# Three drains of TensorE in each pass of a gather-and-scatter kernel

## The chip, the core and the metric

The kernel runs on one core of one Trainium2 chip. The metric is the device time of one execution in microseconds, as the median of several runs. The engines are named as the profile names them: PE is TensorE's matrix unit (PEld its weight loads), DVE is VectorE, ACT is ScalarE, POOL is GpSimd, and SP is SyncE, whose queue issues most DMAs.

## What is computed

One layer of a graph network with 12500 nodes and 400000 edges, 128 features each, in float32:

```python
h = jnp.maximum(_layernorm(x, axis=-1), 0.0)
# inside the layer, on that h:
h = h @ W_in2f.T
Wij = smu(f_ij @ W_f1.T + b_f1) @ W_f2.T + b_f2     # f_ij: 400000 x 20
Wij = Wij * rcut_ij[:, None]
x_ij = h[idx_j] * Wij                                # gather by dst
agg = jax.ops.segment_sum(x_ij, idx_i, num_segments=h.shape[0])   # sum by src
out = smu(agg @ W_o1.T + b_o1) @ W_o2.T + b_o2
x = x + out
```

`smu` is a smooth activation; the kernel makes it from Gelu and a linear term. The edges are sorted by dst, so 128 neighbouring edges read few rows of h. Their src is in no order.

## The kernel before

The edges are cut into 3125 tiles of 128. Four tiles make a group (`GRP`), two groups a super (`SUP`), and one pass of the main loop works on four successive groups at once, each at another stage. There are 782 groups, so 782 passes. The nodes are cut into 98 bins of 128 (`NB`). The messages of the edges go in two steps: first every message row is scattered to DRAM, into a buffer sorted by bin; later the rows of a bin are fetched again and summed on TensorE. The supers are cut into ten epochs (`PARTS`). While one epoch's messages are scattered, an earlier epoch's are summed, bin by bin, with three DRAM buffers in turn.

The order of the instructions on PE, DVE, ACT and SP is the order in which the code writes them (`manual_schedule`). Each engine goes through its list in order, and the framework puts semaphores between them. In pass p the loop (lines 1139 to 1174) calls these helpers:

- `turn` of group p (L707): four 128x128 transposes of the messages `mt` into the PSUM tile `pt`. For the groups that are kept aside (the last two epochs, from `EARLY` on) it is a product with `w_o1` (L709) instead.
- `send` of group p: ScalarE writes the row's place in its bin into the last column of `ms` (L718 or L720), then copies the four transposes out of `pt`, scaled by the edge weight (L723). GpSimd scatters each of the four tiles with one indirect DMA (L738). `ms` has six buffers. Groups from `EARLY` on are stored in order instead (L725) and scattered after the loop.
- `number` of group p+1: VectorE makes the four columns of scatter addresses `ix` (L620).
- `weigh` of p+1 (L686): the second filter product, 512 columns, into `pw`; it reads `sm`.
- `gather` of p+1 (L667): a one-hot product that picks the rows of h, into `ph`.
- `take` of p+1 (L675): ScalarE copies `ph` to `hg`.
- `parts`, first half: some products that sum an earlier epoch's bins (`pg`, L799), about ten a pass in all.
- `mix` of p+1 (L696): VectorE makes `mt` from `pw` and `hg`.
- `hide` of p+2 (L633): the first filter product into `pu`; `bend` (L641): ScalarE's Gelu `ge` of it; `smooth` (L649): VectorE's `sm` from both.
- `count` of p+2 (L578, L580, L581): three products that count, for each edge, its place in its bin, into `pc`; `read` (L608): VectorE takes them out as `sl`.
- `pick_part` of p+3 (L531, L532): ScalarE's one-hot tile `oh`; `bins` of p+3 (L564): VectorE's `so`, four steps that count on.
- `parts`, second half.

Each of `pt`, `pw`, `ph`, `pu` and `pc` has one PSUM buffer. So TensorE's transposes of the next group wait until ScalarE's copies (L723) have read `pt`, and they wait for `mt`. The sums' products need rows that SP has fetched (L769) and a comparison `se` of VectorE (L783); when a set of bins is done, VectorE adds it to `agg` (L812).

After the loop the kept groups are loaded and scattered while the last epochs are summed; then the output products, the old x and the bias are added and stored. A branch with a slow general form (`flag > 0`) stands behind and isn't taken with these inputs.

Of the kernel before, what the change touches and what calls it, by code (L numbers as in the profile page):

```python
# [43 lines left out]
def gnn_kernel(  # L44
# [19 lines left out]
    nc = tc.nc  # L64
# [239 lines left out]
    with tc.tile_pool(name="ld", bufs=4) as ld, \  # L304
# [173 lines left out]
        def at(p):  # L478
            return seq[p] if p < len(seq) else NG

        def sup_at(p):
            return flow[p] if p < len(flow) else NS
# [5 lines left out]
        def load(s):  # L488
            if s >= NS:
                return  # L490
            t0, nt = sups[s]
            e0, n = t0 * P, nt * P
            fb = fbufs[place_of[s] % NF]
            if s > 0:
                nc.sync.dma_start(fb[0:R, :n], f_t[:, e0:e0 + n])
            loaded[s] = (fb,)
            if s > 2:
                targets(s)
# [38 lines left out]
        def s_of(g):  # L537
            return g // PER
# [32 lines left out]
        def count(g):  # L571

            if g >= NG:
                return
            n = groups[g][1]
            before, so = bins_of.pop(g)
            pc = ps1.tile([P, GRP, P], F32, name="pc")[:, :, 0:NB]
            nc.tensor.matmul(pc[:, :n], tri, so[:, :n], start=True, stop=False, skip_group_check=True)  # L578
            if n > 1:
                nc.tensor.matmul(pc[:, 1:n], rest_h, so[:, :n - 1], start=False, stop=False, skip_group_check=True)  # L580
            nc.tensor.matmul(pc[:, 0], rest_h, before, start=False, stop=True, skip_group_check=True)  # L581
            counts[g] = pc
            if g + 1 == BY:
                pt = ps1.tile([P, GRP * P], F32, name="ph")[:, :NB]
                nc.tensor.matmul(pt, ones_h, so[:, n - 1], start=True, stop=True)
                mm = cnt.tile([P, 2], F32, name="mm")
                nc.vector.tensor_reduce(mm[:, 0:1], pt[:, :NB - 1], op=ALU.max, axis=AX.X)
                nc.vector.tensor_scalar(bad[:, 3:4], mm[:, 0:1], float(ZMIN[0]), None, op0=ALU.is_gt)
            if g + 1 in first or g + 1 == NG:

                k = epoch[g // PER]
                pt = ps1.tile([P, GRP, P], F32, name="ph")[:, 0, :NB]
                nc.tensor.matmul(pt, ones_h, so[:, n - 1], start=True, stop=True)
                mm = cnt.tile([P, 2], F32, name="mm")
                nc.vector.tensor_reduce(mm[:, 0:1], pt, op=ALU.max, axis=AX.X)
                nc.vector.tensor_reduce(mm[:, 1:2], pt[:, :NB - 1], op=ALU.min, axis=AX.X)
                i = 4 + 2 * k
                nc.vector.tensor_scalar(bad[:, i:i + 1], mm[:, 0:1], float(CAP[k]), None, op0=ALU.is_gt)
                nc.vector.tensor_scalar(bad[:, i + 1:i + 2], mm[:, 1:2], float(ZMIN[k]), None, op0=ALU.is_lt)
# [11 lines left out]
        def number(g):  # L611
            if g >= NG:
                return
            (t, n), k = groups[g], epoch[g // PER]
            t0, hic = begins[k]
            if s_of(g) < EARLY:
                ix = cnt.tile([P, GRP], I32, name="ix", bufs=8)
            else:
                ix = ix_kept[:, t - kept_tile:t - kept_tile + n]
            nc.vector.scalar_tensor_tensor(ix[:, :n], slots.pop(g)[:, :n], BIG + CAP[k] - 1, hic[:, t - t0:t - t0 + n],  # L620
                                           op0=ALU.min, op1=ALU.add)
            taken[g] = ix
# [21 lines left out]
        def smooth(g):  # L644
            if g >= NG:
                return
            n = groups[g][1] * P
            sm = edge.tile([P, GRP * P], F32, name="sm")
            nc.vector.scalar_tensor_tensor(sm[:, :n], units_of.pop(g)[:, :n], LIN, hidden[g][:, :n],  # L649
                                           op0=ALU.mult, op1=ALU.add)  # L650
            hidden[g] = sm
# [3 lines left out]
        def gather(g):  # L655

            if g >= NG:
                return
            n = groups[g][1] * P
            o = g % PER * GRP * P  # L660
            oh, hw = onehot[g // PER], loaded[g // PER][2]
            ph = ps1.tile([P, GRP * P], F32, name="ph")
            if g // PER < FEW // SUP:
                for q in range(3):
                    nc.tensor.matmul(ph[:, :n], hw[:, q * D:(q + 1) * D], oh[:, o:o + n], start=(q == 0), stop=(q == 2))
            else:
                nc.tensor.matmul(ph[:, :n], hw[:3 * WIN, g % PER, :], oh[:3 * WIN, o:o + n], start=True, stop=True)  # L667
            rows_of[g] = ph

        def take(g):  # L670
            if g >= NG:
                return
            n = groups[g][1] * P
            hg = edge.tile([P, GRP * P], F32, name="hg")
            nc.scalar.activation(hg[:, :n], rows_of[g][:, :n], AF.Copy)  # L675
            rows_of[g] = hg
# [23 lines left out]
        def turn(g):  # L700

            n = groups[g][1]
            pt = ps1.tile([P, GRP, P], F32, name="pt")
            mt = mixed.pop(g)
            for j in range(n):
                if s_of(g) < EARLY:
                    nc.tensor.transpose(pt[:, j, :], mt[:, j * P:(j + 1) * P], ident)  # L707
                else:
                    nc.tensor.matmul(pt[:, j, :], mt[:, j * P:(j + 1) * P], w_o1, start=True, stop=True)  # L709
            mixed[g] = pt  # L710

        def send(g):

            t, n = groups[g]
            ms = msg.tile([P, GRP, ROW], F32, name="ms")
            m = epoch[s_of(g)] // BUFS
            if m:
                nc.scalar.activation(ms[:, :n, P], lo_b[:, t:t + n], AF.Identity, bias=mark[:, m:m + 1])  # L718
            else:
                nc.scalar.activation(ms[:, :n, P], lo_b[:, t:t + n], AF.Copy)  # L720
            pt = mixed.pop(g)
            for j in range(n):
                nc.scalar.activation(ms[:, j, 0:P], pt[:, j], AF.Copy, scale=w_sb[:, t + j:t + j + 1])  # L723
            if s_of(g) >= EARLY:
                nc.scalar.dma_start(kept_rows[:, t - kept_tile:t - kept_tile + n, :], ms[:, :n, :])  # L725
                return
            scatter(g, ms)

        def scatter(g, ms):

            ix = taken.pop(g)
            for j in range(groups[g][1]):
                scatter_tile(g, ms, ix, j)
# [103 lines left out]
        def parts(upto):  # L837
            nonlocal done
            while done < upto:
                add(summing, *work[done])  # L840
                done += 1
# [236 lines left out]
        def step():  # L1078

            nonlocal taken_steps, slot, apart_by  # L1080
            if opening:
                apart_by += 1
                if apart_by % 2 == 0:
                    opening.pop(0)()
                return
            slot += 1
            while taken_steps < COUNT and taken_steps * 3 * (eps_of[0][1] * PER - 22) < slot * COUNT:
                steps[taken_steps]()
                taken_steps += 1
# [49 lines left out]
        for p in range(len(seq)):  # L1139
            g = seq[p]  # L1140
            s = g // PER
            if p == (FEW // SUP - 3) * PER:
                assert not opening
            if p % PER == 0:
                load(sup_at(p // PER + 3))
            if s < EARLY:
                k = chores(g)
            else:
                lo = hi = done
            if p > 1 and p != SLACK:  # L1150
                turn(at(p - (p > SLACK)))
                send(at(p - (p > SLACK)))
            step()
            number(at(p + 1))
            weigh(at(p + 1))
            gather(at(p + 1))
            take(at(p + 1))
            parts(lo + (hi - lo) // 2)
            mix(at(p + 1))
            if p == 0:  # L1160
                turn(at(1))
                send(at(1))
                pick_part(at(2))
            step()
            hide(at(p + 2))
            bend(at(p + 2))
            count(at(p + 2))
            smooth(at(p + 2))
            pick_part(at(p + 3))
            bins(at(p + 3))  # L1170
            read(at(p + 2))
            parts(hi)
            step()
            assert k == 0 or taken_steps == COUNT
# [282 lines left out]
```

## Time and profile before

| | us |
|---|---|
| median of 3 runs (5183.92 to 5208.39) | 5191.76 |
| the profiled execution | 5192.84 |
| its span in the trace | 5190.7 |
| its mean granted TensorE clock | 0.887 |
| busy: PE / PEld / DVE / ACT / POOL | 3896.6 / 2442.9 / 3349.5 / 2957.4 / 3042.1 |

A timeline row has the start, the time, the engine, the source line, the operation, what it writes and reads, how many like it follow each other, and in brackets the idle time of the engine before it with what ended that idle time. "issue" there means that nothing which the profile shows ended it, "remote" that a semaphore ended it which the profile can put down to no instruction. Ends of PE's rows are modelled; the starts are recorded. A row with a count (x4) has the first one's start and the time that all of them cover. In the stage table the figures behind the window are its length, then the busy time of PE, PEld, DVE, ACT and POOL, each with its number of instructions, then the granted clock, the DMA engines' share and GB/s.

### The profile page before, as it was taken

The page shows a single profiled execution, that of the slowest core. Times are in us where ns is not written, and L with a number is a line of the kernel's source. Part 1 is how long each engine was busy: PE and PEld are TensorE (multiplying, and loading weights), DVE is VectorE, ACT ScalarE, POOL GpSimd, SP SyncE. Part 2 cuts the span into 40 slices and gives each one's busy share as a digit, 9 for nine tenths or more (in the row PEclk, how much of TensorE's full clock was granted, in tenths as well). Part 3 has the DMA queues.
Part 4 walks back from the last instruction along what each step waited for, and adds up shares of the span by engine and source line. Part 5 has one row for each costly group of instructions (what it writes and reads, how often), then busy time and mean ns, then how long its engine had stood idle before and what let it go on. Part 6 is the DMA issues. An engine that isn't in the chain of part 4 may idle for free.

```text
span 5190.7 us, 69995 instructions
## 1 busy us (share of the span) xinstructions
PE 3896.6 (75%) x18475; PEld 2442.9 (47%) x18475; DVE 3349.5 (65%) x7364; ACT 2957.4 (57%) x7286; POOL 3042.1 (59%) x3170
## 2 busy tenths in 40 slices
PE   7667767777777777777777777777778877777456
PEld 3233334444444444444444444545455555545446
DVE  6675656666666666666666666666667767667236
ACT  6567866666565565666566666655556655555001
POOL 5666665555555555555565555555656665555554
PEclk9888888988898989989898989999989999989678
DMA  5644434544444443343444344444444444444566
GB/s 158 169 138 139 141 112 147 145 146 145 139 133 122 117 118 116 118 119 115 116 125 117 118 118 131 128 129 127 124 131 145 143 128 147 140 122 147 191 195 199
DMA packets 509824, 708.03 MB, mean 136 GB/s; under 512 B 174382, under 2 KB 362815, under 8 KB 509289
## 3 DMA queue, kind: packets, MB, share of 16 engines
q1 hardware_dynamic: 401992, 484.14, 33.2%
q0 software_dynamic: 100112, 207.06, 12.1%
q10 hardware_dynamic: 7312, 12.29, 0.6%
q8 instruction: 147, 2.41, 0.2%
q14 instruction: 261, 2.13, 0.2%
HBM read 409.48 MB, written 293.71 MB: 135 GB/s over the span
## 4 chain that ended last, share of the span: by engine, by line
PE 49%; DVE 17%; ACT 12%; issue 11%; another core or an unknown queue 10%; DMA 1%; ACTq 0%; POOL 0%; DVEq 0%; POOLq 0%
PE pw L686 14%; PE pg L799 13%; PE pu L633 10%; ACT ms L723 5%; DVE mt L696 5%; DVE sm L649 4%; PE ph L667 3%; DVE se L783 3%; PE pt L707 3%; ACT hg L675 3%; ACT ge L641 2%; DVE so L564 2%; PE pc L581 1%; PE pc L578 1%
## 5 line engine op out<-in xcount | busy, mean ns | idle before, releaser
L738 POOL DMA_INDIRECT buf<-ms,ix x2944 | 2826.0, 960 | 1974.5 <-ACT ms L723 1196.9
L686 PE MATMUL pw<-sm,w_f 128*128 128x512 f32 x1562 | 1024.6, 742 | 771.9 <-DVE sm L649 479.1
L799 PEld LDWEIGHTS pg<-se,rw 128*128 128x128 f32 x8036 | 1153.0, 207 | 450.6 <-issue 372.6
L799 PE MATMUL pg<-se,rw 128*128 128x128 f32 x8036 | 1245.6, 295 | 134.1 <-issue 101.3
L723 ACT ACTIVATE ms<-pt,w_sb 128x128 f32<-128x128 f32 x3121 | 879.5, 363 | 816.5 <-PE pc L581 294.4
L696 DVE SCALAR_TENSOR_TENSOR mt<-pw,b,hg 128x512 f32<-128x512 f32 x781 | 584.0, 748 | 790.5 <-ACT hg L675 585.8
L564 DVE SCALAR_TENSOR_TENSOR so<-irow_ps,hi_f,so 128x98 f16<-128x98 f32 x2936 | 931.4, 317 | 80.3 <-DVE so L564 2.3
L633 PE MATMUL pu<-f,w_f 128*128 128x512 f32 x1562 | 904.6, 664 | 0.0
L641 ACT ACTIVATE ge<-pu 128x512 f32<-128x512 f32 x781 | 472.2, 605 | 740.3 <-remote 224.0
L649 DVE SCALAR_TENSOR_TENSOR sm<-pu,ge 128x512 f32<-128x512 f32 x781 | 535.0, 685 | 477.0 <-ACT ge L641 269.3
L686 PEld LDWEIGHTS pw<-sm,w_f 128*128 128x128 f32 x1562 | 261.2, 210 | 926.6 <-DVE sm L649 553.0
L707 PE MATMUL pt<-ident,mt 128*128 128x128 f32 x2940 | 468.0, 283 | 266.6 <-ACT ms L723 208.7
L675 ACT ACTIVATE hg<-ph 128x512 f32<-128x512 f32 x781 | 472.6, 605 | 289.5 <-PE ph L667 85.2
L783 DVE TENSOR_TENSOR se<-irow_ps,rw 128x1536 f32<-128x1536 f32 (+1 forms) x345 | 587.9, 1704 | 71.9 <-remote 28.3
L532 ACT ACTIVATE oh<-oh,onesb 128x512 bf16<-128x512 bf16 x780 | 562.6, 721 | 26.2 <-ACT oh L531 0.9
L531 ACT ACTIVATE oh<-rbc,nrow 128x512 bf16<-128x512 uint8 x762 | 553.3, 726 | 0.0
L707 PEld LDWEIGHTS pt<-ident,mt 128*128 128x128 f32 x2940 | 341.8, 145 | 312.9 <-ACT ms L723 243.2
L608 DVE TENSOR_REDUCE sl<-pc 128x4 f32<-128x392 f32 x782 | 435.5, 557 | 67.1 <-PE ph L667 22.9
L667 PE MATMUL ph<-oh,hw 126*128 126x512 bf16 x762 | 337.7, 443 | 0.0
L633 PEld LDWEIGHTS pu<-f,w_f 128*128 128x128 f32 x1562 | 292.2, 221 | 81.3 <-issue 66.1
L812 DVE TENSOR_TENSOR agg<-agg,pg 128x512 f32<-128x512 f32 (+1 forms) x200 | 134.4, 672 | 281.2 <-remote 178.1
L578 PE MATMUL pc<-so,tri 128*128 128x392 f16 x736 | 254.4, 346 | 20.6 <-DVE sl L608 13.6
(218 smaller groups left out, 2120.6 us busy)
## 6 DMA issues: line engine op xcount, KB each, us to landing
rw<-buf SPq DMA_DIRECT2D x292, 774.0 KB
buf<-zero SPq DMA_DIRECT2D x146, 387.0 KB
rbc<-rel_dram SPq DMA_DIRECT2D x389, 128.0 KB
buf<-ms,ix POOLq DMA_INDIRECT x2944
rw<-buf SPq DMA_DIRECT2D x49, 645.0 KB
f<-in_f_t SPq DMA_DIRECT2D x390, 80.0 KB
hw<-h_dram SPq DMA_DIRECT2D x762, 31.5 KB
kept_rows<-ms ACTq DMA_DIRECT2D x45, 258.0 KB
```

What stands on the lines that cost most here:

```text
L564: nc.vector.scalar_tensor_tensor(so[:, j], irow_ps[:, :NB], hi_f[:, t + j:t + j + 1], so[:, j - 1] if j else before, op0=ALU.is_equal, op1 ...
L633: nc.tensor.matmul(pu[:, :n], w_f1, loaded[g // PER][0][:, o:o + n], start=True, stop=True)
L641: nc.scalar.activation(ge[:, :n], units_of[g][:, :n], AF.Gelu, scale=ZS)
L649: nc.vector.scalar_tensor_tensor(sm[:, :n], units_of.pop(g)[:, :n], LIN, hidden[g][:, :n], op0=ALU.mult, op1=ALU.add)
L675: nc.scalar.activation(hg[:, :n], rows_of[g][:, :n], AF.Copy)
L686: nc.tensor.matmul(pw[:, :n], w_f2, hidden.pop(g)[:, :n], start=True, stop=True)
L696: nc.vector.scalar_tensor_tensor(mt[:, :n], pws.pop(g)[:, :n], b2, rows_of.pop(g)[:, :n], op0=ALU.add, op1=ALU.mult)
L707: nc.tensor.transpose(pt[:, j, :], mt[:, j * P:(j + 1) * P], ident)
L723: nc.scalar.activation(ms[:, j, 0:P], pt[:, j], AF.Copy, scale=w_sb[:, t + j:t + j + 1])
L738: i = nc.gpsimd.indirect_dma_start(out=bufs[k][:, :], out_offset=bass.IndirectOffsetOnAxis(ap=ix[:, j:j + 1], axis=0), in_=ms[:, j, :], in ...
L783: nc.vector.tensor_tensor(se[:, a:a + n], own.unsqueeze(1).to_broadcast([P, n, P]), rows_in[c][:, a:a + n, P:P + 1].to_broadcast([P, n, P] ...
L799: nc.tensor.matmul(pgs[0][:, g, :], rows_in[c][:, o, 0:P], sel[c][:, o, :], start=(q == 0), stop=(q == Q[k] - 1))
```

## The change

Three drain instructions are put into TensorE's stream in each pass: behind the transposes (`turn`), behind the gathered product (`gather`), and behind the counts (`count`) ahead of the second half of the sums. The first is left out in the passes in which `turn` is not called in this place. TensorE's other instructions and their waits, and those of the other engines, stand in the same order as before.

```diff
@@ -1149,11 +1149,13 @@
                 lo = hi = done
             if p > 1 and p != SLACK:
                 turn(at(p - (p > SLACK)))
+                nc.tensor.drain()
                 send(at(p - (p > SLACK)))
             step()
             number(at(p + 1))
             weigh(at(p + 1))
             gather(at(p + 1))
+            nc.tensor.drain()
             take(at(p + 1))
             parts(lo + (hi - lo) // 2)
             mix(at(p + 1))
@@ -1165,6 +1167,7 @@
             hide(at(p + 2))
             bend(at(p + 2))
             count(at(p + 2))
+            nc.tensor.drain()
             smooth(at(p + 2))
             pick_part(at(p + 3))
             bins(at(p + 3))
```

## The prediction

> **What bounds the kernel now.** I read the page first.
>
> ```profile
> span 5190.7 us, 69995 instructions
> PE 3896.6 (75%) x18475; PEld 2442.9 (47%) x18475; DVE 3349.5 (65%) x7364; ACT 2957.4 (57%) x7286; POOL 3042.1 (59%) x3170
> PE 49%; DVE 17%; ACT 12%; issue 11%; another core or an unknown queue 10%; DMA 1%; ACTq 0%; POOL 0%; DVEq 0%; POOLq 0%
> L738 POOL DMA_INDIRECT buf<-ms,ix x2944 | 2826.0, 960 | 1974.5 <-ACT ms L723 1196.9 <-issue 573.0 <-ACT hg L675 81.9
> L799 PEld LDWEIGHTS pg<-se,rw 128*128 128x128 f32 x8036 | 1153.0, 207 | 450.6 <-issue 372.6 <-DVE agg L812 32.9 <-PE pg L799 2.1
> L707 PE MATMUL pt<-ident,mt 128*128 128x128 f32 x2940 | 468.0, 283 | 266.6 <-ACT ms L723 208.7 <-DVE mt L696 32.4 <-issue 20.8
> ```
>
> The profiled execution took 5192.84 us, 0.02% over the median 5191.76 of the three timed runs; the sum below is made against it. No engine is full, so a wait must set the pace. A tenth of the chain is a wait that the profile can't name, and POOL loses 1197 us to `ms L723`, the scaled copy of the transposes that `send` makes on ScalarE. So next I asked what those copies wait for (us, times) and who waits for them.
>
> ```profile
>   PE pc L581: 294.4, 92
>   remote: 241.4, 68
>   PE pg L799: 120.3, 39
>   PE pu L633: 76.0, 32
>   PE ph L667: 66.7, 44
>   PE pt L707: 6.9, 13
>   POOL buf L738: 1196.9, 513
> ```
>
> Of TensorE's products the first copy of a group needs one alone, the group's last transpose (`pt L707`). Yet only 13 waits end there. 275 waits, 798.8 us, end at a later product or at something unknown. The timeline around one of them says why.
>
> ```profile
> 2618.04 1.13 PE L686 MATMUL pw<-sm,w_f 128*128 128x512 f32 x2 [1.21 <-issue]
> 2621.60 0.60 PE L707 MATMUL pt<-ident,mt 128*128 128x128 f32 x4
> 2622.10 1.12 PE L686 MATMUL pw<-sm,w_f 128*128 128x512 f32 x2
> 2622.59 0.28 ACT L718 ACTIVATE ms<-lo_b,mark 128x4 f32<-128x4 bf16 x1
> 2623.07 0.38 PE L667 MATMUL ph<-oh,hw 126*128 126x512 bf16 x1
> 2624.45 0.97 POOL L738 DMA_INDIRECT buf<-ms,ix  x1 [0.31 <-issue]
> 2624.93 0.90 PE L799 MATMUL pg<-se,rw 128*128 128x128 f32 x6
> 2626.98 1.14 ACT L723 ACTIVATE ms<-pt,w_sb 128x128 f32<-128x128 f32 x4 [4.10 <-remote]
> 2627.62 0.96 POOL L738 DMA_INDIRECT buf<-ms,ix  x1 [2.21 <-ACT ms L723]
> 2628.18 0.66 PE L707 MATMUL pt<-ident,mt 128*128 128x128 f32 x4 [2.35 <-ACT ms L723]
> 2629.31 0.68 DVE L649 SCALAR_TENSOR_TENSOR sm<-pu,ge 128x512 f32<-128x512 f32 x1
> 2630.05 1.32 PE L686 MATMUL pw<-sm,w_f 128*128 128x512 f32 x2 [1.22 <-DVE sm L649]
> 2630.55 1.12 ACT L723 ACTIVATE ms<-pt,w_sb 128x128 f32<-128x128 f32 x4
> ```
>
> The transposes are recorded as ended at 2622.20. ScalarE is free at 2622.87 and starts its copies at 2626.98, 4.8 us behind them. TensorE meanwhile runs through a pass, up to the next transposes, which need the buffer that the copies read. I call this a hold: the product is made, the report of it does not come. While it lasts TensorE works ahead, and that work is finished when the report comes.
>
> What starts and ends a hold? In this one POOL's last scatter ended at 2625.42 and the report came 1.5 us later. Two further places show what TensorE's own pace has to do with it.
>
> ```profile
> 2602.80 0.90 PE L799 MATMUL pg<-se,rw 128*128 128x128 f32 x6
> 2602.95 1.14 ACT L723 ACTIVATE ms<-pt,w_sb 128x128 f32<-128x128 f32 x4 [2.20 <-PE pc L581]
> ...
> 4831.80 0.37 PE L799 MATMUL pg<-se,rw 128*128 128x128 f32 x1 [2.43 <-issue]
> 4841.48 0.95 POOL L738 DMA_INDIRECT buf<-ms,ix_kept  x1 [0.30 <-issue]
> 4847.94 0.69 DVE L812 TENSOR_TENSOR agg<-agg,pg 128x512 f32<-128x512 f32 x1 [38.33 <-remote]
> ```
>
> At 2602.95 the report came while TensorE was in the middle of six matmuls. In the last stage POOL scatters without a pause to 4842.43; TensorE then stands 2.43 us before a single matmul, with nothing named that it waits for, and VectorE gets its sum 5.5 us after POOL stopped. Pauses of TensorE did not bring the reports there; the end of POOL's run did. Last, a stretch in which POOL pauses, and stage means (window, PE, PEld, DVE, ACT, POOL busy, granted clock, DMA):
>
> ```profile
> 2680.62 0.60 PE L707 MATMUL pt<-ident,mt 128*128 128x128 f32 x4
> 2682.08 1.12 ACT L723 ACTIVATE ms<-pt,w_sb 128x128 f32<-128x128 f32 x4
> 2682.70 0.96 POOL L738 DMA_INDIRECT buf<-ms,ix  x1 [8.20 <-ACT ms L723]
> ...
> 2618.04:2622.10 4.06, 4.06 (x22) 2.66 (x22) 3.26 (x9) 3.45 (x10) 3.04 (x4) 1.00 0.21 61
> 390.00:4797.00 4407.00, 3397.92 (x16066) 2112.07 (x16066) 2912.24 (x6341) 2684.09 (x6644) 2590.44 (x2700) 0.90 0.44 130
> 4797.00:5191.00 394.00, 233.73 (x1512) 204.08 (x1512) 166.73 (x212) 38.11 (x67) 217.82 (x218) 0.76 0.63 195
> ```
>
> After 8.2 us without scatters the copies follow the transposes (ended 2681.22) with no idle time of ScalarE. So a full-speed TensorE alone makes no hold. A pass that waits for nothing is 4.06 us of TensorE, and POOL's four scatters are 4 x (0.96 + 0.30) = 5.04; the loop takes 4797/782 = 6.13 a pass. The holds are the difference.
>
> **The change, part by part.** The loop runs 782 passes; the drain behind the transposes is left out in three of them: 779 + 782 + 782 = 2343 drains. Nothing is moved, no semaphore or transfer is added. I read a drain so that TensorE's next instruction goes off only when the earlier ones are through; what counts as through no row shows.
>
> *A drain outside a hold.* No row shows one in the loop. Its price is what overlaps now. Four transposes take 0.60 and one 0.283, so they follow each other by (0.60 - 0.28)/3 = 0.11, and 0.17 of the last one lies under its follower. To this comes the start: `sm` ended at 2629.99 and `pw` began at 2630.05, 0.06. Together 0.23. Where the next weight load can't go ahead either, 0.207 more: 0.44. A gain is excluded for the drain itself, as it only withholds instructions. I take 0.3 (the weight load partly overlaps, as `pw` starts with its own), 0.9 a pass, bounds 0.7 and 1.3. A free pass becomes 4.06 + 0.9 = 4.96, which POOL's 5.04 still covers: nothing on the path, while with 1.3 it would be 5.36 and 0.3 x 782 = 250 us.
>
> *A drain in a hold.* Queued behind the first drain are `pw` and the gathered product, for which `hg` and `mt` wait; behind the second, half of the sums, `pu` and the counts, for which `ge`, `sm` and `sl` wait; behind the third, the other half and the next transposes. I take it that the drain stands until the held reports are out, since the last stage shows TensorE itself standing at 2.43 us a matmul. Then the work ahead, 2622.10 to 2625.83 or 3.7 us, is no longer done under the hold but after it. First pass after the release: 3.7 + 0.9 + 0.5 for the transposes, so the next copies start 5.1 us after the release, instead of 2630.55 - 2626.98 = 3.57. POOL hides that: its first scatter begins 0.64 after the release and four last to 5.7. Second pass: POOL is 7 us into its run, a new hold begins, and TensorE stands at the third drain. At the release it still has six sums (0.90) and the transposes (0.60, which overlap by 0.2) ahead of the copies, where they now start at once: 1.3 us a hold, and nothing hides it, as POOL has run dry. If it stands at the second drain instead, everything from 2623.45 to 2624.93 and a bubble come on top: 1.3 + 1.5 + 0.3 = 3.1.
>
> The Trainium skill ("PSUM — Partial Sum Buffer", Engine vs sequencer instructions) says that a drain waits for the engine to go fully idle; by that the drain stands through a hold if held reports count as not idle, which no row here shows. By the other reading the sum would be the small one of the second rival below.
>
> Sum: 5192.84 + 275 x 1.3 = 5550 us. With 3.1 throughout it is 6045, with half of the holds caught 5371. I take 1.3, since the sums and the next transposes lie right behind the third drain.
>
> **The rivals.** *The drain brings the reports out* (the other side). If reports wait for TensorE to be idle, every drain is a flush: the holds go, with their 799 us, and the time is 5192.84 - 799 = 4394, which POOL allows (2944/4 = 736 passes of 5.04 are 3709, and 394 for the last stage). For it: the transposes at 2621.60 had no idle time before them and were held, those at 2628.18 had 2.35 us and were not (copies at 2630.55). Against it: the rows at 2602.95 and 4831.80. It decides if the copies start within 0.5 us of the transposes when POOL is more than 7 us into a run.
>
> *The passes are only spread.* Later copies give POOL pauses, and holds become rarer. The pause must exceed the 1.5 us between POOL's stop and the release, which a pass of 4.96 seldom gives. If a third of the holds goes: 5192.84 - 799/3 = 4927.
>
> *The drain waits for matmuls under way alone.* Then only bubbles are paid, and POOL covers most: 0 to 250 us, 5193 to 5440, with 5250 likely.
>
> *The clock falls.* The loop has a granted clock of 0.90. A TensorE that stands for 4 us in each hold may be granted half.
>
> ```profile
> 2630.85:2634.25 3.40, 3.40 (x9) 1.78 (x8) 3.27 (x6) 1.42 (x5) 2.17 (x3) 0.50 0.53 175
> ```
>
> Such a window follows some waits now; 3.4 us at half clock lose 1.7. One more for each hold: 5550 + 275 x 1.7 = 6018. The Trainium skill ("TensorE: Matmul & The Clock Gate", Why this matters for your kernels) warns of idle gaps over about 3 us for this reason; here the half clock comes behind a shorter one, the 2.35 us ahead of 2628.18.
>
> That the drains are not carried out is excluded: they stand in TensorE's stream as written.
>
> **How the numbers follow.** Holds stay and drains stand in them: 0.48. The clock falls as well: 0.06. Bubbles alone: 0.15, of which 0.07 within 0.5%. Reports brought out: 0.20. Passes spread: 0.11. So faster by over 0.5% (about what a measurement of this kernel can tell) 0.20 + 0.11 = 0.31, same 0.07, slower 0.48 + 0.06 + 0.08 = 0.62. The likeliest case's own range is 5300 to 5950. The range, 4600 to 5950, takes in bubbles alone, spread passes and a third of the first rival; outside are 0.13 of that, 0.04 of the clock and 0.03 of the ends.
>
> **What would show it.** Right: `pw`, the sums and the counts have idle time before them that ends with the same event as the copies; `ms L723` still waits 2 to 5 us behind the transposes; POOL's idle time over 1974 us. Wrong: copies start right behind the transposes late in a POOL run, POOL near 5.04 us a pass, the unnamed 10% gone from the chain.

## Result and the profile after

| | us | |
|---|---|---|
| before | 5210.66 | median of 6 runs, 5183.92 to 5230.16 |
| after | 5640.32 | median of 6 runs, 5606.03 to 5672.42 |
| ratio | 1.083 | 95% interval 1.078 to 1.088 |

The kernel became 430 us slower; 5550 was forecast, inside a range of 4600 to 5950. The profiled execution of after took 5672.42 us, the longest of its six runs, so the two profiles differ by some 50 us more than the medians. The page of after, with the rows that answer to those of before:

```profile
span 5670.3 us, 72338 instructions
PE 4276.7 (75%) x18475; PEld 2406.3 (42%) x18475; DVE 3366.6 (59%) x7364; ACT 3039.1 (54%) x7286; POOL 3051.7 (54%) x3170
PE 51%; issue 19%; DVE 16%; ACT 7%; another core or an unknown queue 6%; DMA 0%; SPq 0%; DVEq 0%; ACTq 0%; POOL 0%; POOLq 0%
L738 POOL DMA_INDIRECT buf<-ms,ix x2944 | 2834.9, 963 | 2446.1 <-ACT ms L723 1651.9
L799 PE MATMUL pg<-se,rw 128*128 128x128 f32 x8036 | 1353.8, 310 | 809.2 <-issue 665.1
L723 ACT ACTIVATE ms<-pt,w_sb 128x128 f32<-128x128 f32 x3121 | 883.1, 364 | 396.2 <-PE pt L707 291.4
```

Three of these rows as they were before:

```profile
L799 PE MATMUL pg<-se,rw 128*128 128x128 f32 x8036 | 1245.6, 295 | 134.1 <-issue 101.3 <-DVE agg L812 32.2
L686 PE MATMUL pw<-sm,w_f 128*128 128x512 f32 x1562 | 1024.6, 742 | 771.9 <-DVE sm L649 479.1 <-issue 182.8 <-DVE mt L696 81.7
L723 ACT ACTIVATE ms<-pt,w_sb 128x128 f32<-128x128 f32 x3121 | 879.5, 363 | 816.5 <-PE pc L581 294.4 <-remote 241.4 <-PE pg L799 120.3
```

The span grew by 479.6 us (5670.3 - 5190.7), and POOL's idle time ahead of its scatters by 471.6 (2446.1 - 1974.5), while its busy time stayed (2834.9 against 2826.0). So nearly the whole loss shows as longer or more frequent pauses of POOL, and POOL pauses for `ms L723`. The chain's "issue" rose from 11% to 19%: that is how a drain that stands looks in these rows, TensorE waiting for nothing that the profile names. Of TensorE's idle time of this kind 665 us lie ahead of the sums (L799), against 101 before. What the copies themselves wait for (us, times) has turned over:

```profile
  PE pt L707: 291.4, 244
  remote: 75.8, 41
  PE pt L709: 19.9, 13
  issue: 6.9, 8
```

Before, the copies' waits ended at products made after the transposes, since TensorE had run ahead. Now they end at the transposes (`pt L707`), 244 times against 13: TensorE can't run ahead, and the transposes are what is late. The stages (window, PE, PEld, DVE, ACT, POOL busy, clock, DMA):

```profile
390.00:5270.00 4880.00, 3759.07 (x16091) 2083.00 (x16090) 2936.09 (x6368) 2778.90 (x6675) 2610.54 (x2712) 0.90 0.39 117
5270.00:5670.00 400.00, 242.44 (x1557) 209.40 (x1556) 170.24 (x217) 40.42 (x73) 222.40 (x222) 0.76 0.63 195
```

The last stage takes 400 us against 394; the loss is in the loop, at the same granted clock of 0.90. One stretch of its timeline shows a hold at the second drain, a pass that waits for nothing, and a hold at the third drain:

```profile
2617.45 0.47 PE L667 MATMUL ph<-oh,hw 126*128 126x512 bf16 x1
2620.03 0.60 ACT L675 ACTIVATE hg<-ph 128x512 f32<-128x512 f32 x1 [3.14 <-remote]
2620.18 0.96 POOL L738 DMA_INDIRECT buf<-ms,ix  x1 [0.31 <-issue]
2621.47 1.22 PE L799 MATMUL pg<-se,rw 128*128 128x128 f32 x4 [3.54 <-issue]
2626.17 1.12 PE L686 MATMUL pw<-sm,w_f 128*128 128x512 f32 x2
2626.48 1.12 ACT L723 ACTIVATE ms<-pt,w_sb 128x128 f32<-128x128 f32 x4
2627.11 0.96 POOL L738 DMA_INDIRECT buf<-ms,ix  x1 [5.96 <-ACT ms L723]
2629.62 0.93 PE L799 MATMUL pg<-se,rw 128*128 128x128 f32 x6
2630.39 0.60 PE L707 MATMUL pt<-ident,mt 128*128 128x128 f32 x4
2631.10 1.12 PE L686 MATMUL pw<-sm,w_f 128*128 128x512 f32 x2
2634.24 0.21 PE L581 MATMUL pc<-so,rest_h 128*128 128x98 f16 x1
2635.95 0.96 POOL L738 DMA_INDIRECT buf<-ms,ix  x1 [0.30 <-issue]
2638.52 1.64 PE L799 MATMUL pg<-se,rw 128*128 128x128 f32 x6 [4.08 <-issue]
2639.96 1.06 PE L707 MATMUL pt<-ident,mt 128*128 128x128 f32 x4
2641.05 1.14 ACT L723 ACTIVATE ms<-pt,w_sb 128x128 f32<-128x128 f32 x4 [3.28 <-PE pt L707]
2641.70 0.96 POOL L738 DMA_INDIRECT buf<-ms,ix  x1 [4.79 <-ACT ms L723]
```

The counts end at 2634.45 and the six sums behind the third drain start at 2638.52, 1.6 us after POOL's last scatter ended (2636.91). The copies have to wait for these sums and the transposes behind them, and POOL stands for 4.79 us. The sums and the transposes take 1.64 and 1.06 us here against 0.93 and 0.60 at 2629.62 and 2630.39. In the hold at the second drain the reports did not all come at once: ScalarE took the gathered product at 2620.03, ahead of POOL's last scatter, and the sums behind the drain started at 2621.47.

### The profile page after: what moved, and what is told of

It reads as the page before. It is cut to its first block, busy times and chain, and to the rows that moved or that the text cites. A ratio compares the mean times of both kernels' runs of the same rounds, so it can differ in the third digit from the quotient of the medians.

```text
span 5670.3 us, 72338 instructions
## 1 busy us (share of the span) xinstructions
PE 4276.7 (75%) x18475; PEld 2406.3 (42%) x18475; DVE 3366.6 (59%) x7364; ACT 3039.1 (54%) x7286; POOL 3051.7 (54%) x3170
## 4 chain that ended last, share of the span: by engine, by line
PE 51%; issue 19%; DVE 16%; ACT 7%; another core or an unknown queue 6%; DMA 0%; SPq 0%; DVEq 0%; ACTq 0%; POOL 0%; POOLq 0%
PE pg L799 16%; PE pw L686 14%; PE pu L633 9%; DVE so L564 4%; DVE sm L649 4%; PE pt L707 4%; PE ph L667 3%; DVE se L783 3%; ACT ge L641 2%; DVE mt L696 2%; ACT ms L723 1%; DVE sl L608 1%; PE pc L578 1%; PE pc L580 1%
## 5 line engine op out<-in xcount | busy, mean ns | idle before, releaser
L738 POOL DMA_INDIRECT buf<-ms,ix x2944 | 2834.9, 963 | 2446.1 <-ACT ms L723 1651.9
L799 PE MATMUL pg<-se,rw 128*128 128x128 f32 x8036 | 1353.8, 310 | 809.2 <-issue 665.1
L799 PEld LDWEIGHTS pg<-se,rw 128*128 128x128 f32 x8036 | 1104.5, 208 | 1457.3 <-issue 1408.4
L686 PE MATMUL pw<-sm,w_f 128*128 128x512 f32 x1562 | 1022.3, 741 | 348.7 <-issue 130.8
L723 ACT ACTIVATE ms<-pt,w_sb 128x128 f32<-128x128 f32 x3121 | 883.1, 364 | 396.2 <-PE pt L707 291.4
L707 PE MATMUL pt<-ident,mt 128*128 128x128 f32 x2940 | 505.7, 300 | 47.3 <-issue 28.4
L707 PEld LDWEIGHTS pt<-ident,mt 128*128 128x128 f32 x2940 | 387.4, 156 | 78.5 <-issue 55.1
L633 PEld LDWEIGHTS pu<-f,w_f 128*128 128x128 f32 x1562 | 259.9, 209 | 198.2 <-issue 189.0
L667 PE MATMUL ph<-oh,hw 126*128 126x512 bf16 x762 | 323.3, 424 | 0.0
```

The costliest lines, as they stand in the source:

```text
L633: nc.tensor.matmul(pu[:, :n], w_f1, loaded[g // PER][0][:, o:o + n], start=True, stop=True)
L686: nc.tensor.matmul(pw[:, :n], w_f2, hidden.pop(g)[:, :n], start=True, stop=True)
L738: i = nc.gpsimd.indirect_dma_start(out=bufs[k][:, :], out_offset=bass.IndirectOffsetOnAxis(ap=ix[:, j:j + 1], axis=0), in_=ms[:, j, :], in ...
L799: nc.tensor.matmul(pgs[0][:, g, :], rows_in[c][:, o, 0:P], sel[c][:, o, :], start=(q == 0), stop=(q == Q[k] - 1))
```

## The experiments

All runs sent together ran on one chip, with the kernel before beside them. Chips differ much for this kernel: the kernel before took 4038.32 us on the first chip, 5205.19 on the second and 5188.61 on the third, so each experiment is compared with the kernel before on its own chip. The theories are S (a drain stands through a hold, as predicted), F (a fixed price for each drain, wherever nothing covers it) and T (the drain behind the transposes does it all).

**First chip: each drain alone, and two in each place.** Edits against before:

```diff
# e1_transposes
                 turn(at(p - (p > SLACK)))
+                nc.tensor.drain()
# e2_product
             gather(at(p + 1))
+            nc.tensor.drain()
# e3_counts
             count(at(p + 2))
+            nc.tensor.drain()
# e5_doubled: two drains in each of the three places
```

> Only the drain behind the transposes. Theory S (a drain costs nothing by itself, POOL covers it; it stands while TensorE's reports are held, and costs what TensorE still has ahead of the next transposes when the reports come): in the second pass after a release the transposes are already issued when this drain stands, so the copies start at the release as before and the next pass has 5 us of POOL's scatters as cover. 5210 to 5310 us. Theory F (each of the three drains in a pass costs the same, a third of 5640 - 5211): 5354 us. Theory T (the holds show first at the transposes, so this drain catches them and carries nearly all): 5550 to 5640 us.

> Only the drain behind the gathered product. Theory S: the holds begin at the earliest behind the counts or the transposes, so this drain is caught one pass further on, when the copies of the pass before are waiting for the same release and POOL gets them at once; work behind it (sums, first filter product, counts, sums, 3.7 us) then runs under POOL's 5 us. 5210 to 5350 us. Theory F: 5354 us. Theory T: 5210 us.

> Only the drain behind the counts. Theory S: it stands ahead of the sums and the next transposes, which the copies wait for, so the 1.3 us for each of some 275 holds are nearly all here. 5450 to 5600 us. Theory F: 5354 us. Theory T: 5210 to 5260 us.

> All three places, with two drains behind each other in each. Theory S: the second of a pair finds TensorE empty, and POOL covers its own short time, so as the changed kernel: 5620 to 5720 us. Theory F (a drain has a fixed price of 143 us for each place): up to 6070 us.

| | us | ratio | 95% interval |
|---|---|---|---|
| e1_transposes | 4040.02 | 1.0004 | 0.9995 to 1.0014 |
| e2_product | 4088.54 | 1.0123 | 1.0106 to 1.0140 |
| e3_counts | 4038.49 | 1.0000 | 0.9991 to 1.0010 |
| e5_doubled | 4448.74 | 1.1012 | 1.0994 to 1.1031 |

The numbers expected were all for a base near 5200 and miss. The rows say why the base is another one; of e3, then the same two of e5, then `ge` of e1 and of e2:

```profile
L738 POOL DMA_INDIRECT buf<-ms,ix x2944 | 2823.9, 959 | 913.7 <-issue 235.1
L723 ACT ACTIVATE ms<-pt,w_sb 128x128 f32<-128x128 f32 x3121 | 873.8, 360 | 10.2 <-PE pt L707 9.6
```

```profile
L738 POOL DMA_INDIRECT buf<-ms,ix x2944 | 2827.7, 960 | 1321.6 <-ACT ms L723 608.9
L723 ACT ACTIVATE ms<-pt,w_sb 128x128 f32<-128x128 f32 x3121 | 880.1, 363 | 14.2 <-PE pt L707 12.5
```

```profile
L641 ACT ACTIVATE ge<-pu 128x512 f32<-128x512 f32 x781 | 468.6, 600 | 436.6 <-PE pu L633 429.3
```

```profile
L641 ACT ACTIVATE ge<-pu 128x512 f32<-128x512 f32 x781 | 467.2, 598 | 673.1 <-PE pu L633 669.8
```

The copies wait 10 us in all instead of 816.5, with POOL's scatters as many and as long: on this chip reports are not held. POOL's 913.7 us of idle time over 2944 scatters are 0.31 each, the usual space between two. So POOL sets the pace, and a drain alone is covered: the price is nothing in two places. In the third, behind the gathered product, it delays `pu`, for which `ge` waits 673 us against 437 in e1, and 50 us come through. Two drains in each place cost 410 us. The second of each pair lasted 13 ns (the median in each place), so it found TensorE empty, as S had said. But a pass in which nothing is held takes 5.16 us there (`pu` 2600.82 to 2605.98), over POOL's 5.04, so POOL does not cover six drains, which S had expected it to do. The changed kernel itself, three drains a pass, was not run on this chip. The chip thus bears on the first step of the prediction alone, the price of drains without holds. That F's 143 us are paid in each place by itself is out; what holds add had to be asked elsewhere.

**Second chip: what makes the holds, and the drains' own price.** e9_sums_of_x lets the sums fetch parts of x in place of the scattered rows; e6_one_scatter does that and leaves out three of the four scatters of each group in the loop up to `EARLY`; e7 adds the change's three drains to e6; e8 puts three GpSimd copies of 128x512 in place of the three scatters, from the fourth epoch on. In all four the messages are not summed.

```diff
# e9, e6, e7, e8
-    bufs[k][b * CAP[k]:(b + n) * CAP[k], :].rearrange("(b p q) r -> p b (q r)", b=n, p=P))
+    x_flat[0:n * CAP[k] * ROW].rearrange("(b p m) -> p b m", b=n, p=P))
# the same in the second fetch, behind the loop; x_flat is x as one row
# e6, e7, e8
-                scatter_tile(g, ms, ix, j)
+                if j == 0 or s_of(g) >= EARLY:
+                    scatter_tile(g, ms, ix, j)
# e8
+                elif epoch[g // PER] >= BUFS:
+                    nc.gpsimd.tensor_copy(zero[:, 0:GRP * P]..., ms[:, :, 0:P])
```

> The kernel before, with all scatters, but the sums read parts of x instead of the scattered rows (the output is not the layer's). It is the base for the next three. Every theory: as the kernel before, 5150 to 5260 us, with the same 4 to 5 us holds at the copies of the transposes.

> As the base, with one scatter in place of four in each pass of the loop (the other three tiles' rows are left out), no drains. If the holds come from POOL's runs of scatters: no holds, copies start right behind the transposes, and TensorE's free pass of 4.06 us sets the pace: 782 x 4.1 to 4.4 us and 394 for the last stage, 3600 to 3900 us. If TensorE's own pace makes them: holds stay, since TensorE runs as before, and the time stays over 4700 us.

> As e6_one_scatter, with the three drains. Here nothing covers the drains, so this measures their own price: without holds a pass grows by the bubbles, 0.73 us by the rows of the changed kernel (0.9 was predicted): e6_one_scatter plus 500 to 700 us. If a drain costs nothing by itself outside a hold even where TensorE sets the pace: the same as e6_one_scatter.

> As e6_one_scatter, but from the fourth epoch on POOL copies a tile of 128 x 512 three times in place of the three scatters left out, so that POOL is about as busy as before without the DMA work. If POOL's being busy makes the holds: holds come back in the later epochs, passes of about 6 us there. If it is the scatters themselves: no holds, and passes of 4.1 to 5.5 us, as POOL's own time allows.

| | us | ratio | 95% interval |
|---|---|---|---|
| e9_sums_of_x | 5209.64 | 0.9994 | 0.9953 to 1.0035 |
| e6_one_scatter | 3972.21 | 0.7605 | 0.7531 to 0.7678 |
| e7_one_scatter_drains | 4353.68 | 0.8335 | 0.8256 to 0.8413 |
| e8_pool_copies | 4008.55 | 0.7674 | 0.7597 to 0.7751 |

The copies of e9, and of e6 (a line is put in above, so L723 is L724 and so on):

```profile
L724 ACT ACTIVATE ms<-pt,w_sb 128x128 f32<-128x128 f32 x3121 | 879.2, 363 | 724.3 <-PE pc L582 279.2
```

```profile
L724 ACT ACTIVATE ms<-pt,w_sb 128x128 f32<-128x128 f32 x3121 | 873.1, 359 | 9.3 <-PE pt L708 7.7
```

Fetching other rows changes nothing, so the holds don't come from reading what was scattered. With one scatter of four they are gone, on a chip that has them. That they need the run of scatters is thereby shown. Whether it is POOL's issuing them or the transfers that they make is not, as both fell together (POOL's DMA queue moved 61 MB in e6 against 207 before). Nor does e8 settle whether any work of POOL without a pause would do: no hold appeared there either (9.0 us of waits), but POOL was busy only 1631.0 us, 41% of the span, so the run without a pause wasn't there.

e7 against e6 gives the drains' own price where nothing is held and POOL covers nothing: 4353.68 - 3972.21 = 381 us, 0.49 a pass for three, less than the 500 to 700 expected. e6 itself lies above the 3600 to 3900 expected: its last counts start at 3584.0 us, so its 782 passes took 4.58 us each, not 4.1 to 4.4. In e7 they start at 3966.1, 5.07 a pass.

**Third chip: each drain alone where reports are held.** The edits are those of the change (r_after), e1, e2 and e3.

> The changed kernel whole, beside the single drains and the kernel before on one chip. Where the kernel before takes some 5200 us with reports held in most passes (ms waiting 800 us in all): theory S (a drain stands through the hold that it meets, and the copies come late by what TensorE has still to do behind it) 5640 us, 430 above before. Theory F (a fixed price of some 0.5 us a pass for three drains, paid wherever nothing covers it) 5200 + 780 x 0.5 = 5590 at most, and split evenly over the single drains. Where the kernel before takes 4040 us with no reports held: by both theories a pass of 4.93 us of TensorE lies still under POOL's 5.04, and passes differ, so 4040 to 4250; two drains in each place took 4449 there.

> Only the drain behind the transposes. Where reports are held in most passes: theory S 5200 to 5350, since the copies' own report is met by this drain with nothing late behind it that the copies wait for. Theory F 5200 + 780 x 0.17 = 5330. A third theory, T (the drain behind the transposes alone moves the hold, since it stands next to the copies' report): 5640, all of the change. Where no reports are held: 4040 by both S and F, as it was in the earlier run.

> Only the drain behind the gathered product. Where reports are held in most passes: theory S 5200 to 5400, since most of the time in drains of the changed kernel stood at the third one and little here, but with the third gone the holds may be met by this one, with gates, first counts, sums and transposes still to come behind it: 3.1 us a hold for those that it meets. Theory F 5330. Where no reports are held: 4090, as in the earlier run.

> Only the drain behind the first counts. Where reports are held in most passes: theory S 5450 to 5650, the greater part of the change's 430 us, since this is where TensorE stands when the hold is on, with six sums and the next transposes still to be made when it ends. Theory F 5330, the same as each of the others. Theory T 5200. Where no reports are held: 4040, as in the earlier run.

| | us | ratio | 95% interval | above before |
|---|---|---|---|---|
| r_after | 5648.09 | 1.0876 | 1.0782 to 1.0969 | 459 |
| r_e1 (transposes) | 5400.28 | 1.0381 | 1.0287 to 1.0476 | 212 |
| r_e2 (product) | 5363.92 | 1.0334 | 1.0224 to 1.0443 | 175 |
| r_e3 (counts) | 5551.74 | 1.0693 | 1.0600 to 1.0786 | 363 |

The drain behind the counts costs most, 363 of 459 us by itself; S has that in its range, F (5330 for each) and T (5200) do not. But the other two aren't free: r_e1 is above S's 5200 to 5350, and 212 + 175 + 363 = 750, far over 459. r_e2 decides nothing, as it fits both S's 5200 to 5400 and F's 5330; r_after is just above F's 5590 at most (its interval begins at 5594). That the sum is so far over 459 fits S: a hold is met by the drain that stands where it begins, and one only can meet it. Where TensorE stands in r_e3 and in r_e1:

```profile
L799 PE MATMUL pg<-se,rw 128*128 128x128 f32 x8036 | 1351.8, 312 | 984.3 <-issue 928.8
L686 PE MATMUL pw<-sm,w_f 128*128 128x512 f32 x1562 | 1024.5, 744 | 175.2 <-DVE sm L649 92.0
```

```profile
L686 PE MATMUL pw<-sm,w_f 128*128 128x512 f32 x1562 | 1042.2, 754 | 1214.0 <-DVE sm L649 539.4
L799 PE MATMUL pg<-se,rw 128*128 128x128 f32 x8036 | 1278.6, 301 | 122.1 <-issue 88.0
```

Before, TensorE waited 134 us ahead of the sums and 772 ahead of `pw`. With the drain behind the counts it waits 984 ahead of the sums and 175 ahead of `pw`; with the one behind the transposes it is the other way round, 122 and 1214. The wait lies behind the drain, wherever that is put.

The drains' own records settle that it is the holds that make them stand. Counted over each trace is how often a drain ended more than 1 us after the modelled end of the last matmul ahead of it: 253 times in r_e3 (1027 us), 299 in r_e1 (900 us) and 177 in r_e2 (457 us), but never in e3, e1 and e2, the same kernels on the chip that holds no reports. There nine drains in ten ended within 0.05 us. A hold in r_e3 from its timeline:

```profile
2623.23 0.21 PE L581 MATMUL pc<-so,rest_h 128*128 128x98 f16 x1
2625.07 1.14 ACT L723 ACTIVATE ms<-pt,w_sb 128x128 f32<-128x128 f32 x4 [4.18 <-remote]
2625.34 0.93 PE L799 MATMUL pg<-se,rw 128*128 128x128 f32 x6 [1.91 <-issue]
```

The copies and the sums behind the drain are let go within 0.27 us of each other, though neither waits for the other: here the drain ends with the event that lets the reports out. Few holds look like this one: in 28 of the 253 the copies start within 0.3 us of the drain's end. By S the copies are seldom due at that moment, since the sums and transposes that they follow still lie behind the drain.

How the price comes about is seen in POOL's rows, counted over each trace: pauses of over 1.5 us between two scatters (all 3125, those of the kept rows too), and how many scatters stand between two pauses. Before and after are the two profiles of the result; r_after is the changed kernel on the chip of the single drains.

| | pauses | us in all | mean | after 4 scatters | after 8 |
|---|---|---|---|---|---|
| before | 386 | 1234 | 3.20 | 46 | 283 |
| after | 472 | 1695 | 3.59 | 210 | 198 |
| r_after | 474 | 1652 | 3.48 | 219 | 186 |
| r_e1 | 460 | 1435 | 3.12 | 202 | 186 |
| r_e2 | 401 | 1388 | 3.46 | 100 | 222 |
| r_e3 | 383 | 1503 | 3.92 | 72 | 215 |
| e1_transposes | 2 | 9 | | | |

Before, POOL mostly runs through two passes (8 scatters) and then pauses. The drain behind the counts leaves the number of pauses and makes each 0.7 us longer, as S says. The drain behind the transposes makes them no longer, but there are 74 more, and 202 come after a single pass. The whole change does both. 461 us (1695 - 1234) of pauses are added in this table, about the 472 by which POOL's idle time grew: 86 more pauses at 3.20 are 275, and 472 that are 0.39 longer are 184. Two pauses after one pass in after:

```profile
2211.17 1.12 ACT L723 ACTIVATE ms<-pt,w_sb 128x128 f32<-128x128 f32 x4
2211.80 0.96 POOL L738 DMA_INDIRECT buf<-ms,ix  x1 [1.80 <-ACT ms L723]
2215.31 0.60 PE L707 MATMUL pt<-ident,mt 128*128 128x128 f32 x4
2215.59 0.96 POOL L738 DMA_INDIRECT buf<-ms,ix  x1 [0.30 <-issue]
2217.66 1.14 ACT L723 ACTIVATE ms<-pt,w_sb 128x128 f32<-128x128 f32 x4 [1.46 <-remote]
2217.73 1.12 PE L686 MATMUL pw<-sm,w_f 128*128 128x512 f32 x2 [1.82 <-DVE sl L608]
2218.30 0.96 POOL L738 DMA_INDIRECT buf<-ms,ix  x1 [1.75 <-ACT ms L723]
2221.95 0.60 PE L707 MATMUL pt<-ident,mt 128*128 128x128 f32 x4
2224.25 1.14 ACT L723 ACTIVATE ms<-pt,w_sb 128x128 f32<-128x128 f32 x4 [1.41 <-remote]
```

The transposes end at 2215.91, POOL's last scatter at 2216.55, and copies and `pw` start together 1.1 us later. TensorE stands at the first drain with nothing run ahead, so the next pass starts from the same point and ends in the same way at 2224.25: 6.5 and 6.6 us a pass, where 4.93 would do.

## Why the prediction was right, and where it was not

**The price outside a hold: right for one pass, but not that POOL covers it.** The free pass was to become 4.96 us; the one in the stretch above is 4.93 (`pw` 2626.17 to 2631.10). Three drains cost 0.49 us a pass in the mean of e7, under the lower bound of 0.7; a part of their price goes there into waits that TensorE had anyway (`pw` waits 315 us for `sm` in e6 and 102 in e7). That POOL covers one drain where nothing is held is shown by e1 and e3 on the first chip; e2 leaks 50 us. "Nothing on the path" does not stand for all three. The 4.06 us that the sum starts from were a short pass: with nothing held and few scatters the mean is 4.58 in e6, and 5.07 with the drains in e7, over POOL's 5.04, and POOL scatters in 736 of the 782 passes only. In e1, where POOL sets the pace, the last counts start at 3708.7 us, in e7 at 3966.1. So an estimate, from two chips, of what the three drains cost where nothing is held is 257 us. The prediction put this term at nothing.

**A drain stands through a hold: right.** TensorE stood 4.08 us ahead of the sums at 2638.52, and they started 1.6 us behind POOL's stop, against the 1.5 seen before; where no reports are held, no single drain stood over 1 us. By that the rule in the Trainium skill ("PSUM — Partial Sum Buffer", Engine vs sequencer instructions), that a drain waits for full idleness, takes in held reports.

**It stands at the third one: right for the greater part.** r_e3 alone gives 363 of 459 us. In after TensorE stood for over 1 us at the third drain 176 times (547 us), at the first 104 times (185 us) and at the second 53 times (118 us). The stretch at 2621.47 shows the second drain too, where POOL stood 5.96 us.

**275 holds at 1.3 us: a total near the truth from a wrong split, and so by luck.** 357 us was the sum, and r_e3, which the term describes best, lost 363. But there 383 pauses grew by 0.7 us each, 269 us in all (1503 - 1234), of the 331 by which POOL's idle time grew:

```profile
L738 POOL DMA_INDIRECT buf<-ms,ix x2944 | 2835.3, 963 | 2305.3 <-ACT ms L723 1520.5
```

There were more pauses than the 275 waits of the copies that were counted as holds, and each grew by less than 1.3 us.

**"POOL hides that": the step that failed.** The first pass behind a release was to be covered, with copies 5.1 us after it and a new hold only in the second pass. Behind the release at 2217.66 they come 6.6 us after it: the transposes, through 4.9 us after the release, are already caught by the new run. That a new hold begins only when POOL is 7 us into its run does not stand; it had scattered for 4.3 us when these transposes ended. Pauses after one pass went from 46 to 210, and the 86 more pauses in all are 275 us of the pauses added, more than half. r_e1 against r_e3 shows that most of it is the first drain's doing; that the work no longer done ahead is the reason is argued from the rows, not shown by a run.

**The rivals.** Reports brought out by the drain: out, as POOL's idle time rose and TensorE stood idle 4.08 us without getting one. Passes spread: out, since there are more pauses, not fewer. Matmuls under way alone: out where reports are held, since drains stood there and not on the first chip. The price of that rival, bubbles, is paid all the same, and it is not small: TensorE's busy time, with modelled ends, grew by 380 us in after (3896.6 to 4276.7) and by 379 in e7 against e6 (3465.7 to 3844.4), where nothing is held. That is 0.16 us a drain, about the 0.17 of overlap that the prediction counted as lost. That holds add to it is shown for a single drain (363 us in r_e3, nothing in e3). How much of the 430 us of all three is this price and how much the standing no run separates, since the changed kernel was not run where nothing is held. The clock: the mean of after is 0.880 against 0.887, so no; but it is 0.860 in r_e3, where a transpose takes 314 ns against 283, so part of the 363 us there may be a slower clock. Inside a long hold it counts too. At 2638.52 the sums and transposes took 1.2 us more than at 2629.62, behind 4.08 us of standing, while these windows, with standing of 1.8 us in each, kept the full clock (third figure from the end):

```profile
2211.80:2218.30 6.50, 4.47 (x23) 2.51 (x22) 5.91 (x13) 3.76 (x10) 3.84 (x4) 1.00 0.71 216
2218.30:2224.90 6.60, 4.62 (x24) 2.58 (x23) 3.27 (x8) 3.78 (x10) 3.85 (x5) 1.00 0.27 69
```

**What would show it.** POOL's idle time over 1974 us came true (2446.1), and the sums stand ahead. `pw` does not: its wait fell from 771.9 to 348.7 us, since the stand moved behind it to the sums. The copies wait less (396.2 us against 816.5), not the 2 to 5 us each that were named, because the transposes they follow are themselves late.

## What to carry to other kernels

An engine that works ahead while another's report is late is buying time; a drain takes that away, even one whose own price lies under another engine's work: the one behind the counts cost nothing where no report was late, and 363 us where they were. And the short prices add up: a cover that hides one drain a pass need not hide three. Ask of a drain what it may stand for, and what is queued behind it when it is let go. Costs of several drains don't add when they catch the same wait: 750 us one by one were 459 together.

## What the runs showed of the hardware

Reports of finished products are held back while POOL scatters without a pause, on the second and third chips of the experiments: the copies wait 724 us in e9, and 10 us in e3 on the first chip. Not every report waits for POOL to stop: one came between two scatters, at 2620.03 in after. On the first chip the kernel before takes 4038 us in place of some 5200, and in e1, run there, POOL has 2 pauses in place of the 386 of before. Why chips differ stays open, as does whether POOL's other work would hold reports too. On the chips with holds the kernel before loses far more to them than the change does (5205 less 4038 are 1167 us, if the chips differ in nothing else), so the cure would lie in POOL's runs: one scatter in four ran in 3972 us, with part of the work left out. No run here does the whole work without holds on such a chip.
